# A conv and Fourier-attention layer pair: the convolution's row sums by VectorE from a channel-major copy of x, the FFN norm on ScalarE, and a new order of steps

## The chip, the cores and the metric

The kernel runs on one core of a Trainium2 chip. Its engines are TensorE (PE in the profile, with its weight loads as PEld), VectorE (DVE), ScalarE (ACT), GpSimd (POOL) and SyncE (SP), which here only issues DMAs. The metric is the device time of one execution in microseconds (us), as a median of runs. Preparing arrays on the host is no part of it.

## The reference

The input x is 32 images of 56 x 56 positions with 96 channels, in float32. Two layers follow each other:

```python
# layer 0: LN over channels, 96 -> 192 (only the first half of xz is used), 3x3 conv 192 -> 96
h = (x - mu) * rsqrt(var + LN_EPS) * ln_w + ln_b
xz = einsum('bhwc,cd->bhwd', h, w_in) + b_in
x1, z = split(xz, 2, axis=-1)
y = conv3x3_same(x1, conv_w) + conv_b
x = x + silu(y)
# layer 1 on tokens t (3136 an image)
t = t + attn(_ln_t(t))      # product to 192, relu, FFT over tokens, diagonal complex
                            # weights with relu, inverse FFT, product to 96
t = t + ffn(_ln_t(t))       # 96 -> 384 -> 96, operands rounded to an 8-bit float
```

The mean of the first norm is folded into the weights, so an image needs only a scale per position, 1/sqrt(var + eps), before the convolution.

## The kernel before

An image is held as 112 partitions of tokens by 28 groups of 96 channels. Steps of several images run interleaved; every step is a small function with a place on an axis of 8 units an image (`put(when, f, *args)` in `plan`, L570 to L657). All steps of all images are sorted by place and issued in that order, and the scheduler that places instructions on each engine starts from it. All loads and stores go through SP's queue.

**The convolution** uses a row transform: each output of four rows is made from six planes of sums of input rows, so that six products with one dimension of the 3x3 filter stand for twelve. `take_in` (L404) takes a loaded chunk `xl` (8 groups of tokens), measures variance with `bn_stats` (`stats`, L134), takes the power -0.5 on POOL (L147) and multiplies x by it into `xa` (L410). `image` (L161) then makes the six planes by a product: `rows6_sb`, a table of row sums, is the moving operand, and `xa` the weights. This transposes tokens to channels at the same time. ACT copies the sums to `img` (L167), two groups a call. `make_seam` (L416) copies the two columns at the join of the image's halves. There is one `img`, shared by all images.

`conv` (L169) makes, for each of three blocks of output channels and three pairs of planes, 48 product instructions on four column blocks of PE. `conv_sums`, `conv_row` (L201) and `conv_silu` put the planes together into four output rows on DVE, writing each with a stride into `s`; `to_tokens` transposes back, `conv_end` adds to `t`.

**The attention** runs `forth` and `forth_a`, a trip through DRAM (`da`), `second` with its parts, `second_w2`, `second_back`, another trip (`de`), `back` and `back_end`. Its norm's deviation is written by DVE into a 97th column of `t` (L447), which `tokens_a` transposes along.

**The FFN** norm (`normal`, L521) makes four groups of tokens a call, half on ACT (L535), half on DVE (L539). `ffn_first` multiplies to 384 channels, in three parts; ACT copies each to 16 bit (L330); `ffn_relu` (L333) adds the bias and clips on DVE (L335) and rounds to 8 bit in a second instruction (L336). `ffn_second` multiplies back.

Of the kernel before, what the change touches and what calls it, by code (L numbers as in the profile page):

```python
# [9 lines left out]

# [25 lines left out]
CB, NR = 32, 3  # L64
HALVES = ((0, 4), (4, NG))
# [6 lines left out]
RD, IDG, RB, IB = range(4)  # L72

# [12 lines left out]
def hybrid_kernel(ctx: ExitStack, tc: tile.TileContext, x, par, spar, cpar, w_in, conv_w, w1, w2, fw1, fb1, fw2, fb2, fa, fb, ib, ia, rows6, out):  # L86
# [23 lines left out]
    rows6_sb = const.tile([N1, 2 * WC * WG], F32, name="rows6_sb")  # L110
# [9 lines left out]
    xas = [const.tile([N1, 8, C + 1], F32, name=f"xa{i}") for i in range(2)]  # L120
    img = const.tile([C + 1, 2, N2 + 2, WC, WG], F32, name="img")
# [12 lines left out]
    def stats(t, kind, b, i):  # L134


        n = t.shape[1]
        name = f"{kind}_{b}_{i}"
        st = stp.tile([N1, n, 3], F32, tag=f"st{kind}", name=f"st_{name}")
        for j in range(0, n, 2):  # L140
            nc.vector.bn_stats(
                st[:, j : j + 2].rearrange("p j s -> p (j s)"), t[:, j : j + 2, :C].rearrange("p j c -> p c j")
            )
        var = stp.tile([N1, n], F32, tag="var", name=f"var_{name}")
        nc.vector.tensor_scalar(var, st[:, :, 2], 1.0 / C, EPS, ALU.mult, ALU.add)  # L145
        rs = sums.tile([N1, n], F32, tag=f"rs{kind}", name=f"rs_{name}")
        nc.gpsimd.tensor_tensor(rs, var, mhalf[:, :n], ALU.pow)  # L147
        return st[:, :, 1], var, rs
# [12 lines left out]
    def image(xa, b, g, t0):  # L161

        ps = psq.tile([C + 1, 2, 2, WC * WG], F32, tag="q", name=f"im_{b}_{g}_{t0}")
        for j in range(2):
            nc.tensor.matmul(ps[:, j], xa[:, j, :], rows6_sb, start=True, stop=True)  # L165
        j0 = CT * t0 + g + 1
        nc.scalar.copy(img[:, :, j0 : j0 + CT + 1 : CT].rearrange("c h j k g -> c j h (k g)"), ps)  # L167

    def conv(s, b, r, part):  # L169
# [4 lines left out]
        ps = s[part] = pool.tile([128, 2, 2, CT, WG], F32, tag=tag, name=f"cv_{b}_{r}_{part}")  # L174
        for at, k in enumerate(PAIRS[part]):
            for dx in range(3):
                for t in range(NT):
                    cols = img[:, :, CT * t + dx : CT * (t + 1) + dx, k, :]
                    w = wv[:, k, dx, r * CB : (r + 1) * CB]
                    args = ps[t * CB : (t + 1) * CB, at], w, cols  # L180
                    if at + dx + t == 0:
                        nc.tensor.matmul(*args, start=True, stop=False)  # L182
                        continue

                    with tc.high_priority():
                        tc.keep_in_program_order(nc.tensor.matmul(*args, start=(dx == 0), stop=(dx == 2)))  # L186
        if part == 0:
            m = s["m"] = work.tile([128, 2, 2, CT, WG], F32, tag="m", name=f"m_{b}_{r}")
            nc.scalar.copy(m, s.pop(0))

    def conv_sums(s, b, r):

        m, ps = s.pop("m"), s.pop(1)
        sd = s["sd"] = work.tile([128, 2, 2, 2, CT, WG], F32, tag="sd", name=f"sd_{b}_{r}")
        nc.vector.tensor_tensor(sd[:, 0], m, ps, ALU.add)
        nc.vector.tensor_tensor(sd[:, 1], m, ps, ALU.subtract)
        s["y"] = work.tile([128, CT, WG, 4, 2], F32, tag="s", name=f"s_{b}_{r}")
# [3 lines left out]
    def conv_row(s, row, at, scale):  # L201
        y = s["y"][:, :, :, row, :].rearrange("c j g h -> c h j g")
# [10 lines left out]
    def to_tokens(s, b, r, half):  # L213
# [4 lines left out]
        for g in range(g0, g1):  # L218
            nc.tensor.transpose(pt[:, g - g0, :], s[:, g].rearrange("c r i h -> c (r i h)"), ident)  # L219
# [113 lines left out]
    def ffn_relu(h1, hq, b, g, k):  # L333
        h2 = w3.tile([128, G4 * N1], F16, tag="h2", name=f"h2_{b}_{g}_{k}")
        nc.vector.tensor_scalar(h2, h1, b1q[:, k : k + 1], 0.0, ALU.add, ALU.max)  # L335
        nc.vector.tensor_copy(hq[:, k, :], h2, saturate=False)  # L336
# [23 lines left out]
    class Image:  # L360


        def __init__(self, b):
# [3 lines left out]
            self.t, self.s, self.n2t, self.hq = {}, {}, {}, {}  # L367
            self.u, self.at, self.gt, self.gw, self.held = {}, {}, {}, {}, {}
            self.xa, self.xc, self.rs, self.xl, self.y, self.norm = {}, {}, {}, {}, {}, {}
# [24 lines left out]
    def fetch(im, i):  # L394
# [5 lines left out]
        else:  # L400
            im.xl[i] = xnp.tile([N1, j1 - j0, C], F32, tag="xl", bufs=3, name=f"xl_{im.b}_{i}")
            in_turn(im.xl[i], im.tokens[:, j0:j1, :], im.b < 3)

    def take_in(im, i):  # L404

        xl = im.xl.pop(i)
        n = xl.shape[1]
        _, _, rs = stats(xl, "a", im.b, i)
        im.xa[i] = xas[(im.b * len(LN_CHUNKS) + i) % len(xas)]
        nc.vector.tensor_tensor(im.xa[i][:, :n, :C], xl, rs.unsqueeze(2).to_broadcast([N1, n, C]), ALU.mult)  # L410

    def make_image(im, i, j):
        g, t0 = divmod(LN_CHUNKS[i][0] + j, NT)
        image(im.xa[i][:, j : j + 2], im.b, g, t0)

    def make_seam(im):  # L416

        nc.scalar.copy(img[:, 1, 0], img[:, 0, N2])
        nc.scalar.copy(img[:, 0, N2 + 1], img[:, 1, 1])
# [24 lines left out]
    def deviation(im, i):  # L444

        _, var, rs = im.rs[i]
        nc.vector.tensor_tensor(im.chunk(i)[:, :, C], var, rs, ALU.mult)  # L447
# [8 lines left out]
    def forth_a(im, g, j2):  # L456
        if g + j2 == 0:
            im.da = dram.tile([N2, 112, H], F32, tag="da", name=f"da_{im.b}")
        if j2 == 0:
            im.u[g] = w3.tile([112, G4, H], F32, tag="u", name=f"u_{im.b}_{g}")  # L460
# [60 lines left out]
    def normal(im, g, j):  # L521
# [3 lines left out]
        if j == 0:  # L525
            im.xc[g] = xnp.tile([N1, G4, C], F8, tag="xn", bufs=2, name=f"xn_{im.b}_{g}")
            if g % 2 == 0:
                im.shift[i] = stp.tile([N1, mu.shape[1]], F32, tag="shift", name=f"shift_{im.b}_{i}")
                nc.vector.scalar_tensor_tensor(im.shift[i], mu, -1.0, rs, ALU.mult, ALU.mult)
        xc = im.xc[g]  # L530
        for j in (j, j + 1):
            at = g % 2 * G4 + j
            t, scale = im.chunk(i)[:, at, :C], rs[:, at : at + 1]
            if j < 2:
# [8 lines left out]
    def ffn_start(im, g):  # L543
        im.held["n3", g] = ffn_tokens(im.xc.pop(g), im.b, g)
# [4 lines left out]
    def ffn_middle(im, g, k):  # L549
        if k == 0:  # L550
            im.hq[g] = w3.tile([128, 3, G4 * N1], F8, tag="hq", name=f"hq_{im.b}_{g}")
        ffn_relu(im.held.pop(("h1", g, k)), im.hq[g], im.b, g, k)
# [17 lines left out]
    def plan(b):  # L570
        im = Image(b)

        def put(when, f, *args):
            order.append((8 * b + when, len(order), lambda: f(im, *args)))
# [12 lines left out]
        for i, (j0, j1) in enumerate(LN_CHUNKS):  # L587
            at = CONV - 2.485 + 0.531 * i
            ahead = 12 if b == 0 else 2.489 - 0.157 * i
            put(CONV - 7.98 + 0.01 * i if b == 1 else at - ahead, fetch, i)  # L590
            put(at - 0.551, take_in, i)
            for j in range(0, j1 - j0, 2):
                put(at + 0.08 * j, make_image, i, j)
# [4 lines left out]
        put(CONV - 0.078, make_seam)  # L598
# [62 lines left out]

    CONV, FIRST, BACK, FFN = -15.042, -8.232, 8.036, 10.805
# [11 lines left out]
    nc.scalar.dma_start(rows6_sb, rows6)  # L674
    for xa in xas:
        nc.gpsimd.memset(xa[:, :, C : C + 1], 1.0)
    nc.gpsimd.memset(img[:, 0, 0], 0.0)
    nc.gpsimd.memset(img[:, 1, N2 + 1], 0.0)
# [53 lines left out]
    dram = ctx.enter_context(tc.tile_pool(name="dram", bufs=2, space=bass.MemoryType.DRAM))  # L732
# [116 lines left out]

def dft_tables():  # L850
# [57 lines left out]
    rows6 = np.zeros((HW, 2, 2, WC, WG))  # L908
    for g in range(WG):
        for i in range(6):  # L910
            r = 4 * g + i - 1
            if 0 <= r < HW:
                for h in range(2):
                    rows6[r, h, h, :, g] = sums[:, i]
    fb, ib = fb[ORDER], ib[..., ORDER]
    tables = fa.reshape(N1, 112), fb.reshape(112, -1), ib.reshape(114, NP, 112), ia, rows6.reshape(N1, -1)
    return [np.ascontiguousarray(a, np.float32) for a in tables]

# [48 lines left out]
```

## Time and profile before

| | |
|---|---|
| median of 3 runs | 3039.4 us (3037.75 to 3047.59) |
| span of the profiled execution | 3036.8 us |
| mean granted TensorE clock | 0.990 |
| bytes moved by DMA | 355.37 MB, mean 117 GB/s |
| share of 16 DMA engines, main queue | 43.5% |
| image product, PE (L165) | 1792 instructions, 321.2 us of overlapping time |
| its weight loads, PEld (L165) | 1792, 264.1 us |
| copy to img, ACT (L167) | 448, 205.5 us |
| scaling of x, DVE (L410) | 128, 108.8 us |
| powers, POOL (L147) | 384, 650.3 us |

The profile is of one execution on the chip. Busy time is time in which an engine works on at least one instruction; a group's own time can overlap that of other groups on PE, whose instructions are pipelined. The chain of waits follows the last instruction back to what released it. A line number is that of the instruction in the kernel, and a tile's name is the program's.

### The profile page before, as it was taken

How to read it: one execution, taken by the hardware profiler on the slowest of the kernel's cores; microseconds unless marked ns; L12 is line 12 of the kernel's file. 1: busy time of each engine (PE TensorE's matmuls, PEld its weight loads, DVE VectorE, ACT ScalarE, POOL GpSimd, SP SyncE). 2: the span in 40 equal slices, each digit the busy share in tenths (PEclk: the TensorE clock that was granted, in tenths of full speed). 3: DMA queues.
4: the chain of work that ended last, by engine and by line, in shares of the span. 5: the costliest groups of instructions: out<-in, count | busy, mean ns of one | idle time of the engine just before them, and what ended most of it. 6: DMA issues, size and time to landing. Idle time of an engine off the chain costs nothing.

```text
span 3036.8 us, 84414 instructions
## 1 busy us (share of the span) xinstructions
PE 2978.4 (98%) x32693; PEld 2445.3 (81%) x32693; DVE 2348.2 (77%) x7248; ACT 2277.4 (75%) x5703; POOL 647.5 (21%) x398
## 2 busy tenths in 40 slices
PE   8999999999999999999999999999999999999997
PEld 7678788888888887888888888888888888888775
DVE  5548777888778887778887778887778887777778
ACT  3467777787777787777787777787777877777877
POOL 2202122222112221122221222221222221121111
PEclk9899999999999999999999999999999999999998
DMA  3533444443454444444444444434444434444443
GB/s 85 144 93 94 117 126 124 118 123 98 121 133 126 117 116 108 122 130 122 123 109 114 125 126 123 127 98 122 124 128 122 123 96 124 129 129 104 113 123 78
DMA packets 495435, 355.37 MB, mean 117 GB/s; under 512 B 329992, under 2 KB 459304, under 8 KB 494808
## 3 DMA queue, kind: packets, MB, share of 16 engines
q1 hardware_dynamic: 493146, 349.24, 43.5%
q8 instruction: 257, 4.21, 0.6%
q10 hardware_dynamic: 1888, 0.74, 0.1%
q14 instruction: 144, 1.18, 0.1%
HBM read 195.73 MB, written 154.14 MB: 115 GB/s over the span
## 4 chain that ended last, share of the span: by engine, by line
PE 88%; DMA 5%; DVE 3%; ACT 2%; issue 1%; POOL 0%; SPq 0%; ACTq 0%; DVEq 0%
PE cv L186 14%; PE ph L232 10%; PE px L256 10%; PE pa L241 9%; PE im L165 7%; PE pe L309 6%; PE pg L299 5%; PE py L317 5%; PE pg L295 5%; PE po L342 4%; PE pf L328 4%; PE cv L182 3%; PE st L219 3%; PE tp_n L158 2%; DMA de<-es 2%; DMA xl<-in_x 1%
## 5 line engine op out<-in xcount | busy, mean ns | idle before, releaser
L186 PE MATMUL cv<-img,wv 97*32 97x196 f32 x13248 | 621.6, 331 | 0.0
L147 POOL TENSOR_TENSOR rs_c<-var_c,mhalf 112x8 f32<-112x8 f32 (+1 forms) x128 | 206.7, 1615 | 1894.1 <-DVE var_c L145 879.1
L186 PEld LDWEIGHTS cv<-img,wv 97*32 97x32 f32 x13248 | 426.8, 109 | 106.9
L235 ACT ACTIVATE h<-ph,rs_b 112x192 f32<-112x192 f32 x896 | 340.1, 449 | 74.1 <-PE ph L232 74.0
L232 PE MATMUL ph<-w1a,n2t 97*112 97x192 f32 x1792 | 381.2, 335 | 2.0 <-ACT n2t L225 0.9
L241 PE MATMUL pa<-h,fa_sb 112*112 112x384 f32 x896 | 372.3, 497 | 0.8 <-ACT h L235 0.8
L330 ACT CAST h<-pf 128x448 f16<-128x448 f32 x672 | 367.5, 567 | 1.1 <-PE pf L328 1.0
L256 PEld LDWEIGHTS px<-fb_sb,at 112*64 112x64 f32 (+1 forms) x3584 | 319.2, 166 | 58.1 <-issue 8.7
L256 PE MATMUL px<-fb_sb,at 112*64 112x112 f32 (+3 forms) x3584 | 353.5, 272 | 8.1 <-DMA at<-da 4.0
L165 PE MATMUL im<-rows_sb,xa 112*97 112x168 f32 x1792 | 321.2, 313 | 2.1 <-DVE xa L410 1.4
L232 PEld LDWEIGHTS ph<-w1a,n2t 97*112 97x112 f32 x1792 | 278.5, 177 | 47.4 <-issue 18.1
L147 POOL TENSOR_TENSOR rs_b<-var_b,mhalf 112x8 f32<-112x8 f32 (+1 forms) x128 | 227.7, 1788 | 397.3 <-DVE var_a L145 310.2
L165 PEld LDWEIGHTS im<-rows_sb,xa 112*97 112x97 f32 x1792 | 264.1, 168 | 33.1 <-issue 15.7
L242 ACT COPY u<-pa 112x384 f32<-112x384 f32 x448 | 226.2, 505 | 75.6 <-PE pa L241 75.4
L272 DVE SCALAR_TENSOR_TENSOR sv<-px,spar_sb,av 128x224 f32<-128x224 f32 (+2 forms) x352 | 152.9, 434 | 151.3 <-ACT av L263 149.8
L336 DVE CAST hq<-h 128x448 fp8e5<-128x448 f16 x672 | 256.1, 386 | 7.5
L335 DVE TENSOR_SCALAR h<-h,b1q 128x448 f16<-128x448 f16 x672 | 220.1, 329 | 40.6 <-ACT h L330 36.1
L299 PE MATMUL pg<-w2x,gt 128*112 128x96 f32 (+1 forms) x1792 | 243.1, 258 | 0.0
L167 ACT COPY img<-im 97x336 f32<-97x336 f32 x448 | 205.5, 461 | 48.6 <-PE im L165 25.8
L299 PEld LDWEIGHTS pg<-w2x,gt 128*112 128x112 f32 (+1 forms) x1792 | 240.8, 178 | 0.0
L261 ACT ACTIVATE av<-px,spar_sb 128x224 f32<-128x224 f32 (+2 forms) x352 | 162.8, 462 | 100.9 <-PE px L256 99.1
L295 PE MATMUL pg<-w2y,gt 128*112 128x192 f32 (+1 forms) x896 | 226.8, 335 | 1.1 <-DVE gt L282 0.7
(121 smaller groups left out, 6197.6 us busy)
## 6 DMA issues: line engine op xcount, KB each, us to landing
da<-u SPq DMA_DIRECT2D x224, 336.0 KB, 3.1
at<-da SPq DMA_DIRECT2D x224, 336.0 KB, 4.2
de<-es SPq DMA_DIRECT2D x448, 84.0 KB, 2.0
y<-de SPq DMA_DIRECT2D x224, 168.0 KB, 2.5
out<-t SPq DMA_DIRECT2D x224, 168.0 KB, 2.6
t<-in_x SPq DMA_DIRECT2D x96, 336.0 KB, 4.4
xl<-in_x SPq DMA_DIRECT2D x93, 336.0 KB, 4.5
t<-in_x SPq DMA_DIRECT2D x32, 168.0 KB, 3.8
```

The source lines that it names most:

```text
L147: nc.gpsimd.tensor_tensor(rs, var, mhalf[:, :n], ALU.pow)
L165: nc.tensor.matmul(ps[:, j], xa[:, j, :], rows6_sb, start=True, stop=True)
L186: tc.keep_in_program_order(nc.tensor.matmul(*args, start=(dx == 0), stop=(dx == 2)))
L232: nc.tensor.matmul(ph[:, j, :], n2t[:, 2 * j2 + j, :], w1a, start=True, stop=True)
L235: nc.scalar.activation(h[:, j], ph[:, j], AF.Relu, scale=rs[:, 2 * j2 + j : 2 * j2 + j + 1])
L241: nc.tensor.matmul(pa, fa_sb, h, start=True, stop=True)
L242: nc.scalar.copy(u[:, 2 * j2 : 2 * j2 + 2, :], pa)
L256: nc.tensor.matmul(px[rows, j], lhs, fb_sb[:, first(p) : first(p + 1)], start=True, stop=True)
L295: nc.tensor.matmul(pg[:, :, j, :], lhs, w2y, start=True, stop=False, skip_group_check=True)
L299: nc.tensor.matmul(pg[:, half, j, :], lhs, w2x, start=False, stop=True, skip_group_check=True)
L330: nc.scalar.copy(h1, pf)
L336: nc.vector.tensor_copy(hq[:, k, :], h2, saturate=False)
```

## The change

**Row sums.** The host adds an array `xc`, a channel-major copy of x: for each half of an image, 96 channels by 28 columns by one line of 58 values (4 times 14 rows, with two zeros). Two steps load it (`fetch_c`). `take_in` now only measures; `scale` takes the power of all 28 groups at once, `turn` transposes it on PE, has ACT copy it and stores it in DRAM, and `fetch_r` loads it from there, the same line to 96 partitions. DVE multiplies (`scaled`) and makes the six planes (`differences`, `ends`, `inner`, `outer`) straight into `img`. The products and copies of `image`, and the seam, are gone. Zero columns and the row of ones are written to `img` once. A pixel's place in the token order changes (`PLACES`), so that `conv_row` writes runs of 14.

**Small operations.** The variance's scale and offset, the deviation and the shift of the FFN norm go from DVE to POOL; all four groups of `normal` go to ACT; the three roundings of a group of the FFN become one instruction.

**Order.** A table `SHIFT` of 114 offsets is added to the places of steps; the steps of the image have new places; some buffers have another number; the scheduler is told of shorter queues (`WINDOW`).

```diff
+    def powers(st, kind, name):
+
+        n = st.shape[1]
+        var = stp.tile([N1, n], F32, tag=f"var{kind}", name=f"var_{name}")
+        nc.gpsimd.tensor_scalar(var, st[:, :, 2], 1.0 / C, EPS, ALU.mult, ALU.add)
...
         nc.gpsimd.tensor_tensor(rs, var, mhalf[:, :n], ALU.pow)
...
-    def image(xa, b, g, t0):
-
-        ps = psq.tile([C + 1, 2, 2, WC * WG], F32, tag="q", name=f"im_{b}_{g}_{t0}")
-        for j in range(2):
-            nc.tensor.matmul(ps[:, j], xa[:, j, :], rows6_sb, start=True, stop=True)
-        j0 = CT * t0 + g + 1
-        nc.scalar.copy(img[:, :, j0 : j0 + CT + 1 : CT].rearrange("c h j k g -> c j h (k g)"), ps)
+    def columns(k, at):
+
+        a = img[:, PLANE[k], at : at + CT + N2, :]
+        part = tuple(a.ap[0])
+        return bass.AP(a.tensor, a.offset, [part, (WG, CT), (N2 * WG, 2), (1, WG)])
...
-                    cols = img[:, :, CT * t + dx : CT * (t + 1) + dx, k, :]
+                    cols = columns(k, CT * t + dx)
...
-        s["y"] = work.tile([128, CT, WG, 4, 2], F32, tag="s", name=f"s_{b}_{r}")
+        s["y"] = work.tile([128, CT, 2, 4, WG], F32, tag="s", name=f"s_{b}_{r}")
...
-        y = s["y"][:, :, :, row, :].rearrange("c j g h -> c h j g")
+        y = s["y"][:, :, :, SLOT[row], :]
...
+    def ffn_round(h2, b, g):
+        hq = w3.tile([128, 3, G4 * N1], F8, tag="hq", name=f"hq_{b}_{g}")
+        nc.vector.tensor_copy(hq, h2, saturate=False)
+        return hq
...
-            im.xl[i] = xnp.tile([N1, j1 - j0, C], F32, tag="xl", bufs=3, name=f"xl_{im.b}_{i}")
+            im.xl[i] = xnp.tile([N1, j1 - j0, C], F32, tag="xl", bufs=2, name=f"xl_{im.b}_{i}")
...
+    def scale(im):
+        _, im.ra = powers(im.sa, "a", f"a_{im.b}")
+
+    def turn(im):
+
+        ps = psum.tile([N2, N1], F32, tag="a", bufs=2, name=f"tr_{im.b}")
+        nc.tensor.transpose(ps, im.ra, ident[:N1, :N1])
+        rt = stp.tile([N2, N1], F32, tag="rt", bufs=2, name=f"rt_{im.b}")
+        nc.scalar.copy(rt, ps)
+        im.rd = dram.tile([2, NT, CT, HW], F32, tag="rd", name=f"rd_{im.b}")
+        for h in range(2):
+            nc.sync.dma_start(im.rd[h].rearrange("t g q -> g t q"), rt[:, h * HW : (h + 1) * HW])
+
+    def fetch_c(im, h):
+
+        im.xc[h] = xcp.tile([C, N2, LINE], F32, tag="xc", name=f"xc_{im.b}_{h}")
+        in_turn(im.xc[h], xc[im.b, h], im.b < 3)
+
+    def fetch_r(im, h):
+        im.rb[h] = xcp.tile([C, N2 * HW], F32, tag="rb", name=f"rb_{im.b}_{h}")
+        nc.sync.dma_start(im.rb[h], im.rd[h].rearrange("t g q -> (t g q)").partition_broadcast(C))
...
+    def scaled(im, h):
+
+        a = view(im.xc[h], 0, (LINE // 2, 2 * N2), (WG + 1, 2), (1, WG))
+        r = im.rb[h].rearrange("c (j i g) -> c j i g", i=2, g=WG)
+        nc.vector.tensor_tensor(a, a, r, ALU.mult)
+
+    def differences(im, h, outside):
...
+        pair = lambda l0, l1: view(x, l0, (l1 - l0, 2), (LINE, N2), (1, WG))
...
+        nc.vector.tensor_tensor(to, plus, minus, ALU.subtract)
+
+    def ends(im, h):
+
+        x, n = im.xc[h], LINE // 2
+        nc.vector.scalar_tensor_tensor(x[:, :, :n], x[:, :, n:], -4.0, x[:, :, :n], ALU.mult, ALU.add)
...
+    def inner(im, h, k):
+
+        x = im.xc[h]
+        b, a = (x[:, :, START[i] : START[i] + WG] for i in (2, 3))
+        nc.vector.tensor_tensor(planes(h, k), a, b, ALU.add if k == 1 else ALU.subtract)
+
+    def outer(im, h, k):
+
+        w = slots(im, h)
+        if k:
+            to = planes(h, k).rearrange("c j g -> c (j g)")
+            nc.vector.scalar_tensor_tensor(to, w[:, 0], 2.0 if k == 3 else -2.0, w[:, 3], ALU.mult, ALU.add)
+        else:
+            to = img[:C, :2, 1 + N2 * h : 1 + N2 * (h + 1), :].rearrange("c k j g -> c k (j g)")
+            nc.vector.scalar_tensor_tensor(to, w[:, 0::2], -4.0, w[:, 1::2], ALU.mult, ALU.add)
...
-        nc.vector.tensor_tensor(im.chunk(i)[:, :, C], var, rs, ALU.mult)
+        nc.gpsimd.tensor_tensor(im.chunk(i)[:, :, C], var, rs, ALU.mult)
...
-            im.u[g] = w3.tile([112, G4, H], F32, tag="u", name=f"u_{im.b}_{g}")
+            im.u[g] = work.tile([112, G4, H], F32, tag="u", name=f"u_{im.b}_{g}")
...
-                nc.vector.scalar_tensor_tensor(im.shift[i], mu, -1.0, rs, ALU.mult, ALU.mult)
+                nc.gpsimd.tensor_tensor(im.shift[i], mu, rs, ALU.mult)
+                nc.gpsimd.tensor_scalar(im.shift[i], im.shift[i], -1.0, 0.0, ALU.mult, ALU.add)
...
-            if j < 2:
+            if j < 4:
...
+            when += sum(SHIFT.get(key, 0) for key in shifts(f.__name__, args))
             order.append((8 * b + when, len(order), lambda: f(im, *args)))
...
+            put(at - 2.551, take_in, i)
...
+        put(CONV - EARLY - 1.2, scale)
+        put(CONV - EARLY - 0.9, turn)
+        for h in range(2):
+            put(CONV - EARLY - 2.6 + 0.1 * h, fetch_c, h)
+            put(CONV - EARLY - 0.8 + 0.1 * h, fetch_r, h)
+        steps = [(f, h, *k) for h in range(2) for f, *k in ((scaled,), (differences, 0), (differences, 1), (ends,))]
+        for i, (f, *args) in enumerate(steps):
+            put(CONV - EARLY + (EARLY - WRITE) / len(steps) * i, f, *args)
+        steps = [(f, h, k) for f, k in ((inner, 1), (outer, 3), (inner, 2), (outer, 4), (outer, 0)) for h in range(2)]
+        for i, (f, *args) in enumerate(steps):
+            put(CONV - WRITE + WRITE / len(steps) * i, f, *args)
...
+    EARLY, WRITE = 6.2, 3.5
...
+WINDOW = (1, 1, 4)
```

## The prediction

> **What bounds the kernel now.** I read the busy shares first, then a table of stages, then the chain of waits, then the groups by line. The page's first part names a candidate:
> ```profile
> PE 2978.4 (98%) x32693; PEld 2445.3 (81%) x32693; DVE 2348.2 (77%) x7248; ACT 2277.4 (75%) x5703; POOL 647.5 (21%) x398
> ```
> A whole-run share hides stages, so the table of stages comes next (columns: window, its length, busy PE, PEld, DVE, ACT, POOL with instruction counts, granted clock, DMA share, GB/s):
> ```profile
> 0.00:20.00 20.00, 11.38 (x60) 11.16 (x61) 9.08 (x31) 4.89 (x10) 7.80 (x16) 1.00 0.60 104
> ...
> 600.00:1500.00 900.00, 896.89 (x9916) 740.04 (x9915) 715.88 (x2212) 697.59 (x1754) 204.13 (x120) 1.00 0.45 119
> 1500.00:2400.00 900.00, 898.85 (x10060) 739.81 (x10059) 713.35 (x2195) 693.27 (x1741) 196.67 (x116) 1.00 0.45 120
> ...
> 3000.00:3037.00 37.00, 25.99 (x159) 15.14 (x159) 31.82 (x108) 22.11 (x51) 6.04 (x4) 0.71 0.27 69
> ```
> In the middle PE is idle 4.3 us of 1800; nearly all its idle time (58.4 us in all) is in the first and last 150 us. The chain of waits says whether that busy PE is really advancing. Cut out around one image call:
> ```profile
> 1479.55 0.19 PE pf L328
> 1479.74 0.57 PE im L165 x4
> 1480.31 0.44 PE st L219 x4
> 1480.75 0.65 PE ph L232 x4
> ```
> Each piece begins where the one before ended: in this stretch PE passes from product to product with no wait, and one call of `image` is worth 0.57 us of PE. The groups give the mean durations, against which I price the edits (columns: line, engine, operation, tiles, shapes, count; busy us, mean ns; idle before):
> ```profile
> L165 PE MATMUL im<-rows_sb,xa 112*97 112x168 f32 x1792 | 321.2, 313 | 2.1 <-DVE xa L410 1.4 <-ACT img L167 0.5
> ...
> L336 DVE CAST hq<-h 128x448 fp8e5<-128x448 f16 x672 | 256.1, 386 | 7.5
> ...
> L535 ACT ACTIVATE xn<-t,shift,rs_c 112x96 fp8e5<-112x96 f32 x448 | 183.6, 484 | 22.7 <-DVE shift L529 22.7
> ...
> L203 DVE SCALAR_TENSOR_TENSOR s<-sd 128x196 f32<-128x196 f32 x384 | 169.2, 526 | 1.3
> ...
> L539 DVE TENSOR_SCALAR xn<-t,st_c,rs_c 112x96 fp8e5<-112x96 f32 x448 | 128.5, 324 | 10.3 <-PE tp_n L156 10.3
> ```
> The same for 350 to 2800 us, with shapes kept apart:
> ```profile
> L147 POOL TENSOR_TENSOR rs_a<-var_a,mhalf 112x8 f32<-112x8 f32 x81 | 154.9, 1923 | 0.0
> ...
> L410 DVE TENSOR_TENSOR xa<-xl,rs_a 112x768 f32<-112x768 f32 x81 | 77.0, 950 | 0.0
> ...
> L282 DVE SCALAR_TENSOR_TENSOR gt<-sv 128x224 f32<-128x224 f32 x188 | 72.5, 386 | 5.8 <-ACT sv L274 5.8
> ...
> L147 POOL TENSOR_TENSOR rs_a<-var_a,mhalf 112x4 f32<-112x4 f32 x27 | 30.4, 1127 | 0.0
> ...
> L282 DVE SCALAR_TENSOR_TENSOR gt<-sv 128x112 f32<-128x112 f32 x27 | 7.1, 264 | 0.0
> ```
> Note that L165's 321.2 us counts overlapping ends of pipelined products; 448 calls by 0.57 us, 255 us, is what the chain shows.
>
> [...] rs_a takes 1.65 us at the quiet start and 1.92 us on average in the middle. [...]
>
> **Part by part, for one image in the middle.** The starts of the seam copy (L418) at 584.94 and 2698.22, 23 images apart, give 91.9 us an image; the best repeat is 91.66. Scaled to that, DVE has 73.0 us of work, ACT 70.9, POOL 20.5.
>
> *PE.* 14 calls of `image` by 0.57 = 8.0 us go. One small transpose (`turn`) comes, two instructions, taken as 0.25 us from tp_n (0.38 us for four). The conv products keep number and width (97x196): 91.7 - 8.0 + 0.25 = 83.9 us.
>
> *DVE, added.* For each of two halves: `scaled` 1568 elements, 1.79 us; `differences` twice 784, 0.97 each; `ends` 812, 1.00; `inner` twice 392, 0.57 each; `outer` twice 392 and once 784. That is 1.79+1.95+1.00+1.13+1.13+0.97 = 7.97, both halves 15.9 us. Segments of 14 are not free for sure: below by nothing, above by L203's price, whose scattered writes cost 526 ns where 112 and 224 elements at L282 give about 356 for 196, that is 1.5 times. I take no surcharge, because the inner runs are contiguous, and keep +8 us an image as the far end.
> *DVE, removed.* xa 108.8/32 = 3.4 us; three kinds of var 57.3/32 = 1.8; deviation 0.6 and shift 0.65 (18.7 and 20.7 over 32); half of `normal` 128.5/32 = 4.0; three casts in one: 21 by 386 ns become 7 by about 853 [...], 2.0 less; L203 now writes runs of 14, 12 by 0.17 = 2.0 less. Sum 14.4. DVE goes to about 74.5 us, 89% of 83.9.
>
> *ACT.* Image copies -6.4 (205.5/32), seam copies -0.7 (21.5/32), 14 more `normal` by 484 ns +6.8, the copy in `turn` +0.3: unchanged at 70.9, 85%.
>
> *POOL.* rs_a -6.7 (215.9/32); one 28-wide power: 0.2 us a column between 4 and 8 wide, 1.92+20*0.2 = 5.9; 21 small operations (var 9, deviation 4, shift 8). Those no row shows: from 0.16 us (as on DVE) to 1.1 (the 4-wide power); I take 0.4, 8.4 in all. About 28 us of 84, hidden behind PE. What they lengthen is var to rs to deviation to tokens_a, some 0.5 us against an order with 0.4 of 8 units (5 us) between norm and first use.
>
> *DMA.* Copies of x by channel, 2 by 609 KB an image, and the broadcasts, 2 by 588 KB: 78 MB more on 355. Rows are 6 KB long while 330,000 of 495,000 present packets are under 512 B, so the share of 45% grows to perhaps 60%: not a bound, but landings get longer. `u` falls from three buffers to two and `xl` from three to two; da<-u lands in 3.1 us against some 10 us between groups, which covers it.
>
> *Moved steps.* Every step has a new place, and with it every DMA on SP: fetches of x earlier, stores earlier, and four new issues an image for scales, of which the broadcast stands on SP until the write has landed (about 2 us, from de<-es). SP waits for its producers already, so I price that wait at 0 to 2 us of PE an image. The new chain is: last statistics, var and power 6.3, transpose and copy 1, write 2, broadcast about 6 (in between 4.4 for 336 KB and 7.7 in proportion): some 15 us. The order leaves about 1.2 units from the last take_in to `scaled`, 12.5 us at 10.5 a unit. DVE may therefore stand about 3 us at `scaled`, with conv sums and ReLU parts queued behind it, for which PE's double PSUM buffers wait. DVE has 9 us of slack an image, so most is absorbed. I take 0.7 us of PE idle an image (now 0.2), bounds 0 and 2.5.
>
> *Start.* Before, the first conv product is at 27.3 us. After, all four chunks must be measured first (about 14 us), then the chain of 15, then DVE's 9.5 (scaled, differences, ends of both halves) and 2.3 for the first two pairs of planes: about 42, so +15 us, bounds +5 and +25. The end has no image work: 0, though four `normal` on ACT at 0.48 could add 5.
>
> **Sum.** Profiled span 3036.8 = 32 by 91.7 + 102. After: 32 by 83.9 = 2685, + 102 + 15 + 32 by 0.7 (22) = 2824. The median shown, 3039.4, lies 2.6 over the span, so 2827.
>
> **Rivals.**
> A. DVE becomes a co-bound: segments dearer by a quarter, or in-order waits, give a period of 86 to 88 us. For: 89% on an in-order engine that also waits. Against: PE ran at 99.7% with DVE at 79%. Time: 32 by 86.5 to 88, + 120 = 2890 to 2940.
> B. Slower than before. Mechanism: the scales arrive late at `scaled`, and DVE stands there in every image, so that conv sums and gates behind it starve PE. It must cost over 7.3 us of PE an image (7.75 saved, less 15/32) to cancel; DVE's slack of 9 us and the doubled PSUM come first, so the chain would have to be some 18 us late: broadcasts landing in 20 us or more behind the larger queue. For: SP's queue is in order and one wait there holds all later loads. Against: DMA at 45%, landings of 2 to 4.5 us. At 10 us: 3115.
> C. Stalls as now and a start hidden by the fill's idle PE: 2785 to 2795.
> D. The PE work does not really leave the path, as the transposes wait elsewhere: no change. Little speaks for it.
>
> **Numbers.** Forecast 0.64 (its own range 2795 to 2870), A 0.20, B 0.10, C 0.04, D 0.02. A measurement tells 0.3%, about 9 us, from no change. Faster 0.88, same 0.02, slower 0.10. Range 2790 to 2905: the forecast, C and the nearer half of A.
>
> **What would show it.** Right: no im group; distance between images 84 to 85 us; DVE near 88% and gapless PE chain; `scaled` near 1.8 us, L203's successor near 360 ns, the triple cast near 850; first conv near 42 us. Wrong: PE under 96% in the middle with waits on DVE or on the broadcast, `scaled` far over 1.8 us, landings over 15 us, or conv products dearer than 2.1 us for 48.

## The result, and the profile after

The changed kernel takes 3279.05 us, the median of 4 runs (3270.09 to 3282.98), beside 3040.84 us before (4 runs, 3037.75 to 3047.59). The ratio is 1.0767, with a 95% interval of 1.0743 to 1.079: 7.7% slower, where 7% faster was forecast. The profiled execution has a span of 3268.3 us at a mean granted clock of 0.948 (before: 3036.8 and 0.990).

The page's first part, busy time with its share of the span, and two rows of the stage table (window, length, busy PE, PEld, DVE, ACT, POOL with counts, granted clock, DMA share, GB/s):

```profile
PE 2945.4 (90%) x30933; PEld 2262.5 (69%) x30933; DVE 2444.8 (75%) x6160; ACT 2250.2 (69%) x5671; POOL 899.8 (28%) x972
```
```profile
600.00:1500.00 900.00, 823.65 (x8707) 634.58 (x8707) 687.24 (x1726) 636.58 (x1605) 262.25 (x272) 0.95 0.52 136
1500.00:2400.00 900.00, 829.83 (x8765) 639.38 (x8764) 691.25 (x1740) 640.50 (x1615) 261.41 (x274) 0.95 0.52 135
```

PE has 1760 instructions less, and yet the middle is not limited by PE any more. It stands still for 76 us in 900 where it stood for 3, and its clock is granted at 0.95 where it was 1.00. No other engine has become the bound: DVE is busy for 687 of 900 us and ACT for 637, both less than before. A kernel in which nobody is full is a kernel that waits. The `turn` copy (L438) starts 17 images apart at 658.96 and 2341.76, so an image takes 98.99 us instead of 91.7.

The waits name two places (engine, line, what it waited for: us in all, times, longest):

```profile
ACT xn L614 <- POOL shift L608: 177.3, 83, 5.0
...
PE pe L324 <- ACT gw L316: 117.3, 30, 4.6
...
DVE xc L462 <- DMA rb<-rd: 89.9, 32, 10.2
```

The last is the wait at `scaled` that the prediction spoke of, 2.8 us an image. The first two, which nobody had on the list, belong together, as the timeline of one image shows (start, length, engine, line, operation; in brackets how long the engine had stood, and who released it):

```profile
1586.75 1.64 POOL L157 TENSOR_TENSOR rs_c<-var_c,mhalf 112x8 f32<-112x8 f32 x1
...
1588.47 5.16 POOL L607 TENSOR_TENSOR shift<-st_c,rs_c 112x8 f32<-112x8 f32 x1
1588.48 0.86 DVE L353 CAST hq<-h 128x1344 fp8e5<-128x1344 f16 x1
...
1590.02 0.36 DVE L218 SCALAR_TENSOR_TENSOR s<-sd 128x196 f32<-128x196 f32 x1
...
1592.60 0.97 DVE L497 SCALAR_TENSOR_TENSOR img<-rb 96x784 f32<-96x784 f32 x1
1593.49 0.35 DVE L147 BATCH_NORM_STATS2 st_a<-xl 112x6 f32<-112x192 f32 x1
1593.72 0.20 POOL L608 TENSOR_SCALAR shift<-shift 112x8 f32<-112x8 f32 x1
1593.95 0.47 ACT L614 ACTIVATE xn<-t,shift,rs_c 112x96 fp8e5<-112x96 f32 x1 [4.42 <-POOL shift L608]
1594.33 0.46 ACT L316 COPY gw<-pg 112x384 f32<-112x384 f32 x1
...
1594.83 1.24 PE L324 MATMUL pe<-gw,ib_sb 112*112 112x96 f32 x8 [3.94 <-ACT gw L316]
```

A product of 112 by 8 numbers, the shift of the FFN norm, lies on POOL for 5.16 us. It begins beside DVE's triple cast, and then DVE runs eight instructions, one straight behind the other, that each read two operands in SBUF (in order L370, a residual add, L297, a gate product, and L218; then L494, L487, L497, L494 and L497, the rest of `inner` and `outer`; two of the eight are shown). It ends at 1593.63, 0.14 us after DVE has begun a `bn_stats`, which reads one operand. All that time ACT stands at `xn`; behind it in ACT's queue is the copy `gw` of the attention, whose operand PE had finished at 1590.9 and which starts at 1594.33, after the first `xn`, and PE stands at `pe`, which needs `gw`. PE is still for 3.94 us, and in the 5 us after it its clock is 0.66. Short stretches of the stage table around the two stalls, same columns:

```profile
1565.00:1570.00 5.00, 2.88 (x17) 2.42 (x17) 4.27 (x10) 2.87 (x7) 0.00 (x0) 0.82 0.77 172
1570.00:1575.00 5.00, 5.00 (x36) 2.78 (x38) 5.00 (x13) 2.48 (x6) 3.35 (x4) 0.50 0.26 72
1590.00:1595.00 5.00, 1.06 (x9) 0.89 (x9) 3.84 (x8) 1.05 (x3) 3.83 (x2) 1.00 0.65 182
1595.00:1600.00 5.00, 5.00 (x24) 3.98 (x25) 0.26 (x1) 3.75 (x10) 0.00 (x0) 0.66 0.14 36
```

In the second and fourth row PE is busy without a gap, at a clock of 0.50 and 0.66, behind the stall in the row above each. In the second pair one pause of 3.94 us goes before: read us by us, the clock is 1.00 until 1595, 0.75 in the next us and 0.50 from 1596 to 1598. In the first pair no pause is as long: PE stands for 1.23 us until 1566.60 and for 0.90 us until 1568.64. It is busy for 1.52 of the 3.00 us from 1565 to 1568, still at 1.00; the clock is 0.59 in the next us and 0.50 from 1569 to 1575. So shorter pauses, close together, went before the same fall; no run shows where the limit lies. The first pair is the other stall. The chain of waits through it (start, length, what):

```profile
1552.30 6.88 DMA rb<-rd
1559.21 1.79 DVE xc L462
...
1563.21 1.78 DVE xc L462
...
1588.47 5.17 POOL shift L607
...
1594.33 0.47 ACT gw L316
1594.83 1.24 PE pe L324 x8
```

DVE waits for the broadcast of the scales, then works off `scaled` and what stood behind it, and PE lacks its gates and sums meanwhile.

**Is it POOL or its neighbour?** The durations of all shift products (min, median, max in ns):

```profile
L607 POOL TENSOR_TENSOR shift<-st_c,rs_c x128: 198/594/5577, 271.5 to 3240.6; 112x8 f32<-112x8 f32 x96, 112x4 f32<-112x4 f32 x32
```

From 350 to 2800 us there are 25 that take over 3 us (4.18 to 5.18), about one an image, the same instruction that takes 0.2 us elsewhere; the whole run has 27, up to 5.58. In all 25 the end goes with the end of such a run on DVE: 20 end 0.13 to 0.16 us after the start of the next `bn_stats`, and 5 about 0.05 to 0.07 us after the last L497. The product lasts much longer than one instruction of the run (0.36 to 0.97 us in the timeline): in all 25 cases it did not end where one instruction of the run followed another without a gap (10 of the 25 begin beside the cast, which reads one operand, and did not end behind that either). That the two SBUF operands of DVE's instructions are what holds POOL is an assumption; the trace shows lengths and ends only. Nor is it a rule for every such pair. In the same run there are places where POOL does end between two of them (start, length, engine, line, operation):

```profile
381.96 0.95 DVE L473 TENSOR_TENSOR rb<-xc 96x784 f32<-96x784 f32 x1
...
382.12 0.86 POOL L155 TENSOR_SCALAR var_c<-st_c 112x8 f32<-112x8 f32 x1 [14.36 <-DVE st_c L147]
...
382.84 0.55 DVE L487 TENSOR_TENSOR img<-xc 96x392 f32<-96x392 f32 x1
```

Both DVE instructions read two operands in SBUF and follow without a gap, and POOL's step ends at 382.98, 0.06 us after the first and long before the second. In the whole run 25 of these variance steps end so behind an L473, and 10 shift products behind an L296. What makes the difference no run shows.

So theory P: the new row sums make long runs of such instructions on DVE, and POOL is kept out of some of them to their end; a step of 0.2 us, moved to POOL, falls into one per image and stalls ACT, then PE. Against it stand the scales' trip (the prediction's rival B, called R in the expectations) and, further on, the order of steps (O), bursts of loads (D), the sheer work of DVE (V), the spectrum's trip through DRAM (F) and the load of `t` (L).

### The profile page after: what moved, and what is told of

It reads as the page before. It is cut to its first block, busy times and chain, and to the rows that moved or that the text cites. A ratio compares the mean times of both kernels' runs of the same rounds, so it can differ in the third digit from the quotient of the medians.

```text
span 3268.3 us, 80704 instructions
## 1 busy us (share of the span) xinstructions
PE 2945.4 (90%) x30933; PEld 2262.5 (69%) x30933; DVE 2444.8 (75%) x6160; ACT 2250.2 (69%) x5671; POOL 899.8 (28%) x972
## 3 DMA queue, kind: packets, MB, share of 16 engines
q1 hardware_dynamic: 509722, 428.09, 50.3%
## 4 chain that ended last, share of the span: by engine, by line
PE 42%; DMA 19%; ACT 14%; DVE 13%; POOL 8%; issue 4%; SPq 1%; ACTq 0%; DVEq 0%; POOLq 0%
PE cv L201 7%; PE px L271 6%; DMA de<-es 5%; PE pa L256 4%; PE pe L324 4%; POOL shift L607 4%; PE ph L247 4%; DMA out<-t 4%; DMA rb<-rd 4%; POOL rs_c L157 3%; PE py L332 3%; ACT xn L614 3%; PE po L360 2%; DMA t<-in_x 2%; PE pg L314 2%
## 5 line engine op out<-in xcount | busy, mean ns | idle before, releaser
L201 PE MATMUL cv<-img,wv 97*32 97x196 f32 x13248 | 658.5, 338 | 0.0
L614 ACT ACTIVATE xn<-t,shift,rs_c 112x96 fp8e5<-112x96 f32 x896 | 378.9, 485 | 177.3 <-POOL shift L608 177.3
L271 PE MATMUL px<-fb_sb,at 112*64 112x112 f32 (+3 forms) x3584 | 419.8, 285 | 28.1 <-DVE sv L290 18.8
L155 POOL TENSOR_SCALAR var_c<-st_c 112x8 f32<-112x8 f32 (+1 forms) x128 | 46.6, 364 | 1182.1 <-DVE st_c L147 1182.1
L157 POOL TENSOR_TENSOR rs_a<-var_a,mhalf 112x28 f32<-112x28 f32 x32 | 153.5, 4798 | 682.1 <-PE tr L436 681.7
L324 PE MATMUL pe<-gw,ib_sb 112*112 112x96 f32 (+1 forms) x1792 | 232.5, 277 | 117.3 <-ACT gw L316 117.3
L324 PEld LDWEIGHTS pe<-gw,ib_sb 112*112 112x112 f32 (+1 forms) x1792 | 220.5, 191 | 146.2 <-ACT gw L316 122.5
L594 DVE TENSOR_TENSOR t<-py,t 112x384 f32<-112x384 f32 x224 | 123.8, 553 | 215.0 <-PE py L332 214.2
L343 PE MATMUL pf<-n3t,w1q 96*128 96x448 fp8e5 x672 | 239.5, 374 | 19.4 <-ACT n2t L240 11.5
L332 PE MATMUL py<-y,ia_sb 113*112 113x384 f32 x448 | 206.5, 546 | 46.3 <-DMA y<-de 29.5
```

Of the source, the lines that this page charges most:

```text
L271: nc.tensor.matmul(px[rows, j], lhs, fb_sb[:, first(p) : first(p + 1)], start=True, stop=True)
L324: nc.tensor.matmul(pe[:, half, j, :], ib_sb[: gw.shape[0], p, :], gw[:, half, j, :], start=True, stop=True)
L332: nc.tensor.matmul(py, ia_sb, y, start=True, stop=True)
L343: nc.tensor.matmul(pf, w1q[:, k * 128 : (k + 1) * 128], n3t, start=True, stop=True)
L614: nc.scalar.activation(xc[:, j], t, AF.Identity, bias=im.shift[i][:, at : at + 1], scale=scale, saturate=False)
```

## The experiments

Where no other is named, a time is a median of at least four runs, and the ratio is to the kernel before, run on the same chip. Each edit also makes the scheduler find another order, so differences of 20 or 30 us between variants can't be put down to the edit alone.

**The shift on DVE again** (`e1_shift_dve`):

```diff
-                nc.gpsimd.tensor_tensor(im.shift[i], mu, rs, ALU.mult)
-                nc.gpsimd.tensor_scalar(im.shift[i], im.shift[i], -1.0, 0.0, ALU.mult, ALU.add)
+                nc.vector.scalar_tensor_tensor(im.shift[i], mu, -1.0, rs, ALU.mult, ALU.mult)
```

> Edit: the shift of the FFN norm is made by one VectorE instruction again, as before the change; all else as after. Theory P (POOL starved: the shift product on POOL waits for the end of a run of VectorE instructions with two SBUF inputs, ACT stands behind it in order, and PE behind ACT's gw): the waits of ACT xn on POOL shift (177 us) go, the waits of PE pe on ACT gw (117 us) fall below 20, granted clock rises above 0.96, and the time falls by about 32 times 5 to 7 us to 3060 to 3120. Theory R (the scales' trip through DRAM and VectorE's backlog set the pace): the time falls by less than 60 us, to over 3210. Theory O (the new order as such is bad): no change beyond 1%.

Measured: 3122.73 us, 1.0262 (1.023 to 1.0293), and 93.7 us an image. Four instructions an image moved between engines take 156 us off, two thirds of all that the change had lost. Its waits from 350 to 2700 us have in that place:

```profile
ACT xn L614 <- DVE shift L607: 37.7, 50, 1.7
```

In the same window of the changed kernel ACT waits 151.4 us at `xn`. The long waits are gone (at most 1.7 us), and with them PE's wait of `pe` for `gw`. P holds for this part.

**Half of the FFN norm on DVE**, the shift still on POOL (`e2_norm_half`): `if j < 4:` at L613 becomes `if j < 2:`.

> Edit: half of the FFN norm goes back to VectorE (j under 2 on ACT, as before the change); the shift stays on POOL. Theory P: ACT still waits for the shift, so the wait of ACT xn on POOL shift stays over 120 us and the time stays within 2% of 3279, although ACT has 6.8 us an image less to do. A theory that ACT has too much work says 3279 falls by over 100 us.

Measured: 3197.07 us, 1.05 (1.0469 to 1.0531). It gains 82 us without touching the shift, more than expected; ACT waits 99.5 us at `xn` in the whole run. With two `xn` instead of four behind each shift, less depends on it, and the order is another, in which only one shift product takes over 3 us (27 in the changed kernel). So the stall was mostly not met here, and the run says little on ACT's load; `e10_e1_half` says more.

**The broadcast without its trip** (`e3_static_r`), reading x, so that the scale before the convolution is left out, and **both edits** (`e4_both`):

```diff
-        nc.sync.dma_start(im.rb[h], im.rd[h].rearrange("t g q -> (t g q)").partition_broadcast(C))
+        nc.sync.dma_start(im.rb[h], x[im.b].rearrange("n c -> (n c)")[: N2 * HW].partition_broadcast(C))
```

> Edit: the broadcast reads the head of x in DRAM in place of the stored scales, so it waits for nothing but its buffer; the planes are then scaled by other numbers (the scale of the conv norm is left out of the result), with every instruction kept. Theory P: only the stall at VectorE's scaled goes (90 us of waits on rb, of which PE sees some 2 to 3 us an image): 3180 to 3230. Theory R: most of the loss goes, 3000 to 3100.

> Edit: both the shift on VectorE and the broadcast from x (the scale of the conv norm left out of the result). If the two stalls are the whole of the loss, PE is over 98% busy in the middle and the time is 2840 to 2920. If the order itself (the table of offsets, the scheduler's short queues) costs more, it stays over 3000.

Measured: 3210.86 us, 1.0551 (1.051 to 1.0592), and for both together 3049.14 us, 1.0019 (1.0003 to 1.0035, 12 runs). Alone the trip costs 68 us, the shift 156; both, 230, so they add. They make up the whole loss against the kernel before, and not the expected gain: 2840 to 2920 was forecast for the two. An image takes 91.2 us where 83.9 was the sum. PE in the middle of `e4_both` is still short of full:

```profile
600.00:1500.00 900.00, 867.08 (x9499) 669.22 (x9498) 745.81 (x1909) 685.93 (x1735) 233.10 (x214) 0.98 0.59 148
```

The next runs look for that rest. `e3_static_r`, where the shift is still on POOL, still has P's stall: from 600 to 2400 us ACT waits 104.3 us at `xn` for the shift, up to 5.4 us at a time (changed kernel: 117.8, up to 5.0).

**No loads of the channel-major copy after the first image** (`e5_both_no_xc`: `xc` is loaded for image 0 alone and used for all).

> Edit: as e4 (shift on VectorE, broadcast from x, the scale of the conv norm left out), and the channel-major copy of x is loaded for the first image only, later images reuse the same tile (their own x is left out of the convolution); 1.2 MB of loads an image less, every other instruction kept. Theory D (bursts in which the DMA engines are full make stores and trips through DRAM land late, on SP's in-order queue): the waits on out<-t, t<-in_x and de<-es shrink, PE in the middle goes over 98% busy and the time to 2850 to 2940. If the rest of the loss lies in the order of steps, it stays over 3000.

Measured: 3037.47 us, 0.998 (0.9966 to 0.9995, 20 runs), 12 us less than `e4_both`. Half of the added traffic is not what holds the kernel: D falls.

**The order** (`e6_e1_no_shifts`: `e1_shift_dve` without adding the table `SHIFT`; `e7_e1_no_window`: with the scheduler's own queue lengths).

```diff
-            when += sum(SHIFT.get(key, 0) for key in shifts(f.__name__, args))
```
```diff
-    with short_window(), tile.TileContext(nc, schedule_with_timeline_sim=True) as tc:
+    with tile.TileContext(nc, schedule_with_timeline_sim=True) as tc:
```

> Edit: e1 with the table of offsets left out (every step at its plain place). Theory O (the table fits another kernel than the chip runs): under 3070. Theories P and D: the table is not the cause, 3100 to 3250.

> Edit: e1 with the scheduler's own queue depths in place of the short ones. Theory O: under 3070, since the scheduler may again move work around a waiting step. Theories P and D: 3080 to 3200.

Measured: 3203.34 us, 1.0529 (1.0497 to 1.0561), and 3510.45 us, 1.1537 (1.1498 to 1.1575). Without the table it is 81 us slower, without the shorter queues 388. The table and the short queues help the new kernel; neither is what made it slow. The new places of the image's own steps were not tried apart.

**The shift on POOL in the kernel before** (`e8_before_pool_shift`), the same two lines, put into L529 of the old kernel.

> Edit: the kernel before, with the shift alone on POOL in two instructions, as the change has it. Theory P: the product on POOL takes long only behind a run of VectorE instructions with two SBUF inputs; the kernel before has no image steps on VectorE, so it stays under 2 us at most places and the time within 1% of 3040. If POOL is simply slow at this, whatever VectorE does, the time rises by 2 to 5% here too.

Measured: 3088.18 us, 1.0146 (1.0117 to 1.0175).

```profile
L529 POOL TENSOR_TENSOR shift<-st_c,rs_c x128: 192/203/789, 228.5 to 3054.6; 112x8 f32<-112x8 f32 x96, 112x4 f32<-112x4 f32 x32
```

The same instruction has a median of 203 ns and never takes 0.8 us beside the old DVE program, which has no row sums. So POOL is not slow, and its 5 us come from the neighbour. The 46 us it costs even here were not expected to be so many. The first half of P, the stretching, holds; that the move would be nearly free in the old kernel doesn't.

**The scales earlier** (`e9_e1_early`: `e1_shift_dve`, with `fetch`, `take_in`, `scale`, `turn` and `fetch_r` 0.7 units earlier).

```diff
-        put(CONV - EARLY - 1.2, scale)
-        put(CONV - EARLY - 0.9, turn)
+        put(CONV - EARLY - 1.9, scale)
+        put(CONV - EARLY - 1.6, turn)
```

> Edit: e1 (shift on VectorE), and take_in, scale, turn and fetch_r of every image 0.7 units (about 8 us) earlier, with the loads of x that take_in reads; nothing is left out. Theory R for the second part of the loss (the scales' trip is too late by some 3 us): the time falls from 3123 to about that of e4, 3030 to 3070. If what e3 and e4 showed was an effect of other timing and not of the trip, it stays within 1% of 3123.

Measured: 3098.38 us, 1.0196 (1.0162 to 1.0231), the best complete version of the changed kernel, but only 24 us of the 74 that leaving the trip out brings. That is within 1% of 3123, which by the expectation speaks for an effect of other timing and against the trip. But the edit took little of the wait away: at L462 DVE stands 69.5 us for `rb` in the whole run, 84.9 in `e1_shift_dve` and 12.0 in `e4_both`. So this run does not bear the trip's cost out, nor does it refute it; the cost rests on `e3_static_r` and `e4_both`.

**Which of the moved small steps were good** (`e10_e1_half`: `e1_shift_dve` and half of the norm on DVE; `e11_image_only`: that, and the variance and the deviation on DVE; `e12_e1_half_early`: `e10_e1_half` with the earlier trip).

```diff
-        nc.gpsimd.tensor_scalar(var, st[:, :, 2], 1.0 / C, EPS, ALU.mult, ALU.add)
+        nc.vector.tensor_scalar(var, st[:, :, 2], 1.0 / C, EPS, ALU.mult, ALU.add)
...
-        nc.gpsimd.tensor_tensor(im.chunk(i)[:, :, C], var, rs, ALU.mult)
+        nc.vector.tensor_tensor(im.chunk(i)[:, :, C], var, rs, ALU.mult)
```

> Edit: e1 with half of the FFN norm on VectorE again: the norm is as before the change, the small operations var and deviation stay on POOL. If ACT standing in order behind xn is a second cause (e2 gave 82 us that theory P had not foreseen), the time falls from 3123 to 3040 to 3090. If e2's gain was only that fewer products waited for POOL, 3110 to 3150.

> Edit: e10 with var and deviation on VectorE too, so nothing of the small work is moved any more: only the row sums, the joined rounding and the order differ from the kernel before. If POOL's small operations still hold up PE (deviation before tokens_a), the time falls below e10 by 20 to 60 us; if they were hidden, it stays within 15 us of e10 or rises by the 3 us an image that VectorE has more to do.

> Edit: e10 with the scales' trip 0.7 units earlier as in e9. If the three causes add (shift, half of the norm, trip), the time is 2960 to 3030, faster than the kernel before (3041); if they share one stall, it is close to the better of e9 and e10.

Measured: 3149.7 us, 1.035 (1.0293 to 1.0406); 3193.45 us, 1.0505 (1.0483 to 1.0527); 3154.0 us, 1.0379 (1.0349 to 1.0409). With the shift on DVE, taking the norm back from ACT costs 27 us, no more than another order can bring, and taking the variance and deviation back from POOL another 44. So of all that moved between engines only the shift is seen to do harm, and that although the variance on POOL is the same sort of small step. The earlier trip brings nothing to this variant, where 2960 to 3030 was forecast if the three causes added; how much of that is the order, no run tells.

**What keeps `e4_both` from its sum.** Four runs start from it. `e13_no_img` makes the row sums for the first image only. `e14_static_y` loads `y` from x, so that nothing waits for the spectrum's way back through DRAM. `e15_no_t` loads `t` for the first image only and overwrites it. `e18_floor` joins these three and leaves out the loads for the row sums too.

```diff
     def scaled(im, h):
+        if im.b:
+            return
```
```diff
-            nc.sync.dma_start(im.y[g][:112], rows[:, g * G4 : (g + 1) * G4, :])
+            nc.sync.dma_start(im.y[g][:112], im.tokens[:, g * G4 : (g + 1) * G4, :])
```

> Edit: e4, and the row sums (scaled, differences, ends, inner, outer) are made for the first image only; later images convolve its planes (their own row sums are left out). All loads, the statistics and all products stay. Theory V (16 us of VectorE work an image, in order ahead of conv sums and gates, is the residual): an image takes 84 to 86 us and the time is 2800 to 2880. If trips and loads are the residual, it stays over 2980.

> Edit: e4, and the inverse transform's operand y is read from x in place of the stored spectrum (its result is left out), so no load of y waits for a store. Theory F: 2850 to 2950. Theory V or L: within 40 us of e4's 3049.

> Edit: e4, and for images after the first x is not loaded into t, the convolution's result is written there alone (the residual x of layer 0 is left out): 1.2 MB less to load an image, and conv_end on VectorE waits for no load. Theory L: 2880 to 2970. Theory V or F: over 3000.

> Edit: e13, e14 and e15 together, and no loads of xc and of the scales after the first image (row sums, the spectrum's return, layer 0's residual and the scales left out for those). All TensorE products stay. If 83.9 us is TensorE's work, an image takes 83.9 to 85 us in the middle. If the floor was set too low, it stays at 86 us or more with PE busy over 99%.

Measured: `e13_no_img` 3138.79 us, 1.0322 (1.0307 to 1.0337); `e14_static_y` 2969.42 us, 0.9768 (0.9751 to 0.9784); `e15_no_t` 3056.59 us, 1.0057 (1.0038 to 1.0075); `e18_floor` 2905.55 us, 0.956 (0.9539 to 0.958).

Without 16 us of DVE work an image, `e13_no_img` is slower in all. The stage table says where: its middle takes 89.7 us an image, 1.5 less, but the loads for the row sums, whose buffers nothing reads any more, run ahead early on, in

```profile
150.00:350.00 200.00, 144.26 (x1525) 106.62 (x1518) 85.55 (x253) 67.14 (x164) 37.50 (x36) 0.81 1.04 256
```

where the DMA share is 1.04, 28 loads of `xc` are issued (14 images' worth) and PE is idle for 56 us of 200. Read from the middle, V and the load of `t` (L) fall, and the spectrum's trip (F) is real: 80 us. How they come about is not shown: from 350 to 2800 us of `e4_both` PE waits for `y` for 8.8 us only, while SP stands 98.5 us for stores of `es` before it can issue loads of `y`. It is a trip that the old kernel had too, but there it was covered. `e18_floor` comes nearest to what PE itself needs:

```profile
600.00:1500.00 900.00, 887.55 (x9992) 698.15 (x9993) 658.03 (x1839) 719.74 (x1843) 208.47 (x226) 1.00 0.42 114
```

With all its products and at full clock PE is busy for 887.55/900 of 86.8 us, 85.6 us, an image.

**Two tries at P from the other side.** `e16_shift_pool_soon` makes the shift on POOL right behind the power, so that it is ready long before `normal`. `e17_gaps` puts a copy of one value, with one SBUF input, between the instructions of `inner` and `outer`, to let POOL in.

```diff
+            nc.gpsimd.tensor_tensor(im.shift[i], mu, rs, ALU.mult)
+            nc.gpsimd.tensor_scalar(im.shift[i], im.shift[i], -1.0, 0.0, ALU.mult, ALU.add)
...
-                nc.gpsimd.tensor_tensor(im.shift[i], mu, rs, ALU.mult)
-                nc.gpsimd.tensor_scalar(im.shift[i], im.shift[i], -1.0, 0.0, ALU.mult, ALU.add)
```
```diff
+        nc.vector.tensor_copy(gap[:, 1:2], gap[:, 0:1])
```

> Edit: the changed kernel with the two shift products still on POOL, but issued right behind the power rs_c, about an image eighth earlier than their use in normal. Nothing is left out. Theory P with place: the wait goes from ACT to nowhere, and the time is near e1's 3123 (3090 to 3150). If POOL at all is too slow for this chain, it stays over 3200.

> Edit: the changed kernel, shift on POOL, nothing left out; before every outer and after every inner on VectorE a copy of one element a partition (one SBUF input, about 0.14 us, 10 an image). Theory P (POOL's product is shut out while VectorE runs back to back through instructions with two SBUF inputs): no shift product over 2.5 us (25 of 4.2 to 5.2 now), the waits of PE pe on gw shrink below 30 us, the time 3110 to 3180 in spite of 1.4 us more VectorE work an image. If the product is slow for another reason, it stays over 4 us once an image and the time over 3270.

Measured: 3264.77 us, 1.0748 (1.0728 to 1.0767), and 3285.73 us, 1.082 (1.0795 to 1.0845). In the first the longest shift is still 5.18 us and ACT waits as long as ever (170.3 us): in the changed kernel POOL already begins each of the 128 shifts 0.08 us behind the power (1588.39 and 1588.47 in the timeline above), and so it does here, so the edit moved nothing and tests nothing. The second tells nothing. The copies depend on nothing, and the scheduler put them elsewhere, as their row shows (last numbers: first and last start in us):

```profile
L494 DVE COPY gap<-gap x192: 124/149/157, 1.2 to 357.8; 96x1 f32<-96x1 f32 x192
```

All are over by 358 us, while 26 shifts of 4.18 us and more come later. Whether a gap in DVE's run would let POOL in was thus not tried.

## Why the prediction was wrong

**The step that failed** is the cost of POOL's small operations: taken as 0.4 us each, bounded at 0.16 and 1.1, "hidden behind PE", lengthening only the way to `tokens_a` by "some 0.5 us". Two things were missed in it. The shift is not on the way to `tokens_a` but ahead of `normal`, which the same change had just made four instructions on ACT, with the attention's copies queued behind them; the prediction named no one behind that wait. And the upper bound of 1.1 us left out what DVE does beside POOL, though the same text had POOL's power at 1.65 us at the quiet start and at 1.92 in the middle, and the same change gave DVE 16 us an image of two-input instructions. Measured: in 27 of 32 images one shift of 4.2 to 5.6 us, and 156 us in all.

**The idle time of PE**, 0.7 us an image with a far end of 2.5, is the term in which this stall and that of the scales' trip had to stand. It was 8.4 us: (900 − 823.65)/900 of 98.99. Nothing at all was set down for the clock, which was lower in the wake of such pauses (0.50 and 0.66 in the two above). PE's busy time is 90.6 us an image after, against 85.6 in `e18_floor`. The difference of 5 us is put down to the clock; that is an estimate, and agrees with what a mean clock of 0.95 leaves out of 99. With the idle time and 1.7 us by which `e18_floor` lies over the sum (below), this is the difference of 15 us from 83.9 to 99.0.

Step by step, from the changed kernel down to the floor (image time; PE idle and PE busy of it, worked out from the window of 600 to 1500 us of each; clock there):

| kernel | us an image | idle | busy | clock |
|---|---|---|---|---|
| changed | 99.0 | 8.4 | 90.6 | 0.95 |
| shift on DVE | 93.7 | 4.7 | 89.0 | 0.97 |
| and no trip of the scales | 91.2 | 3.3 | 87.9 | 0.98 |
| and no trip of the spectrum | 88.6 | 1.9 | 86.7 | 1.00 |
| `e18_floor` | 86.8 | 1.2 | 85.6 | 1.00 |

Each stall taken away is paid back twice, once as idle time and once as clock.

**The removal on PE** was 91.7 − 8.0 + 0.25 = 83.9, and in `e18_floor` PE is busy for 85.6. The 8.0 was right: counted on PE from the start of each product to the start of the next, `image` took 7.9 us an image before (600 to 2400 us). What the sum lacks lies elsewhere. By the same count `turn` takes 0.6 us in `e18_floor`, where 0.25 was set down, the transposes of `t` (`tp_n`) 3.8 us an image where they took 2.8 before, `px` 10.1 for 9.6 and the conv products 19.4 for 19.1, in part as idle time. The median step from one conv product to the next is 8 ns in both, and of `tp_n` 96. So `e18_floor` still holds short waits, and 85.6 us is an upper bound of what PE needs; how far under it one can get was not measured.

**What was right** are the sizes of the instructions. In the groups from 350 to 2800 us:

```profile
L353 DVE CAST hq<-h 128x1344 fp8e5<-128x1344 f16 x172 | 146.8, 853 | 1.8
...
L218 DVE SCALAR_TENSOR_TENSOR s<-sd 128x196 f32<-128x196 f32 x296 | 101.4, 356 | 0.8
...
L462 DVE TENSOR_TENSOR xc<-xc,rb 96x1568 f32<-96x1568 f32 x50 | 89.2, 1784 | 58.6 <-DMA rb<-rd 58.6
```

The cast was put at 853 ns, an estimate that no row of before bore out, the sums in runs of 14 at 356, `scaled` at 1.79 us. The prices of the row sums lie on the line through the two sizes of L410 before (549 ns at 384 elements, 950 at 768), which gives 1785 ns at 1568 elements, 967 at 784, 996 at 812 and 557 at 392. No surcharge for segments came: `scaled` takes 1784, `differences` 958, `ends` 992, `inner` 556. DVE has 75.6 us an image (74.5 forecast), ACT 70.0 (70.9), POOL 28.8 (28). The 28-wide power is 4.80 us (5.9). The DMA share is 50.3% (about 60). The first conv product starts at 40.1 us (42), and fill and end together are 3268.3 − 32·98.99 = 101 us (117).

**The rivals.** B named the scales' trip, and there the wait is what the prediction gave, 2.8 us an image (3). The forecast called it absorbed by DVE's slack; B, as the thing that could starve PE. By `e3_static_r` and `e4_both` against `e1_shift_dve`, it costs 68 to 74 us, over 2 us an image, so it was not absorbed (`e9_e1_early` leaves this open), but B's threshold of 7.3 us was not reached by it. The outcome is on B's side by another mechanism. A (DVE as co-bound) is wrong: DVE is less busy than before, and without its row sums the middle of `e4_both` gains 1.5 us an image. C and D did not happen.

What stays open: `e14_static_y` still has 1.8 us an image more than `e18_floor`, and `e4_both` 2.6 more than that, and no single wait of theirs stands out. They are spread over round trips and the order that each edit makes anew. A version that has the changed work and none of the stalls, about 2900 us by `e18_floor`, was not found.

## What to carry to other kernels

An operation moved to a free engine is priced by who stands behind its result, in order, on each engine down to the bound, and by what its new neighbour does just then, not by its length. When the bound is relaxed, every wait that it used to cover comes into sight, and on PE a pause of 3.94 us, or two of 1.23 and 0.90 close together, was followed by a clock of 0.66 or 0.50 over 5 us, and so paid a second time. So take such a change in parts: here even the small steps that went to POOL differed in sign, 44 us gained by the variance and the deviation, 156 lost by the shift.

## What was unexpected in the hardware

A POOL product of 0.2 us took up to 5.58 us beside a run of DVE instructions most of which have two SBUF inputs, and in the 27 cases of over 3 us in the changed kernel ended with the run, not with one of its instructions. Yet in the trace of the changed kernel 25 variance steps and 10 shift products on POOL ended between two such instructions that followed without a gap. What tells the two apart, how long the product would take beside a longer run, and whether a short gap would end it, no run shows. Beside a DVE program without the row sums, 128 of the same products had a median of 203 ns and a maximum of 789.

The clock of PE fell to 0.50 not only behind a pause of 3.94 us, but also behind 3.00 us in which PE was busy for 1.52, with no pause over 1.23.
